# The order of the nodes worked out inside the loop over h, and x of layers 2 and 3 turned by VectorE and transfers instead of TensorE

## Chip, cores and metric

The kernel runs on one core of one Trainium2 chip. The metric is the device time of an execution in microseconds. A core has five engines that run side by side and wait for each other through semaphores: TensorE (PE; PEld is its weight load), VectorE (DVE), ScalarE (ACT), GpSimd (POOL) and SyncE (SP). SyncE computes nothing; it issues transfers (DMAs). POOL and ACT can issue them too. Each engine executes its queue in order.

## What is computed

Four graph layers run in a row over x of 8 batches, 2048 nodes and 64 features, each followed by a residual sum and a layernorm. All matrices `adj` are the same 2048 x 2048 matrix.

```
x = layernorm(x + L0(x, H, adj))   # attention over 64 hyperedges, mixed with adj/deg @ (x @ W_ind)
x = layernorm(x + L1(x, adj))      # (D^-1/2 (adj + I) D^-1/2) @ x @ W.T
x = layernorm(x + L2(x, adj))      # [x, adj x, adj adj x (combined), softmax(relu(E E.T)) x]
                                   #   times weights of each node = node_embeddings @ weights_pool
x = layernorm(x + L3(x, adj))      # three steps of v = W2 relu(W1 [v, adj v] + b1) + b2
```

The order in which nodes are visited in layer 0 is internal: nodes are sorted by the number of hyperedges they belong to, so that a tile of 128 nodes needs as few slots as possible. Every output must come out in the original order.

## The kernel before

Line numbers are those of the kernel before. The program is built with a scheduler: the source gives the instructions in a program order, and the scheduler places them on the engines by what is ready and by priority, and adds all waits. Instructions wrapped in `keep_in_program_order` (all matmuls by `mm`, all transposes by `transpose`, and those wrapped in `pin`) may not move ahead of what stands before them on their engine. A tile of a pool with a tag and `bufs` buffers waits until the oldest tile of that tag has been released by all its readers.

The four batch pairs (p = 0 to 3) are treated one after the other. x is kept as 16 tiles of 128 nodes with 128 columns (two batches of 64 features). A chunk c is 512 nodes, four tiles. N is 2048, P is 128, JT is 4, NCH is 4, NP is 4.

**Start and loop over h (lines 412 to 621).** From the hyperedge matrix the degree of each node is taken, then its rank (lines 481 to 514), and the ranks are inverted into `order`, the list of nodes for each place (lines 535 to 567): comparisons on DVE, 16 small matmuls into `po`, two DVE instructions. After that the loop over 16 tiles t (line 576) multiplies x by the first weights (`ph`, line 579), forms exponentials on ACT and products `st` and `ex` on DVE, stores `st` to `hs_hbm` every second tile, and adds up `pagg` (line 614). `fetch_rows` (line 256) gathers rows of `hs_hbm` by `order` on GpSimd's queue after the loop.

**Slots, with filler (lines 643 to 785).** The attention of layer 0 is worked out tile by tile. In between, `fill(n)` takes n matmuls from a generator `filler`, here `products()` (line 323), which multiplies x by `adj`. Inside it, `inverses()` (line 340) turns the degrees of `adj` into reciprocals. It gives way 8 times (line 351) before it starts the transposes that spread them. Each matmul of the filler advances a clock by `tick()`; `later(n, f)` and `after(n, f)` run f after n ticks.

**Mixing (lines 848 to 1040).** For 16 steps i (pair and chunk), in each pass of the loop: `mix_scores(i)`, `mix_end(i - 1)`, `mix_load(i + 2)`, `mix_ind(i + 1)`, `mix_g(i + 1)`, `mix_weigh(i)`, with 8 or 9 fills between. `mix_g` (line 864) loads the attention result `gn` and x into `rs[i]` (tag r, two buffers), transposes `gn` on TensorE, and 8 ticks later GpSimd adds `gn` to x (line 879). `mix_end` (line 913) adds the mixed part, normalizes with `normalized` and stores the result to `x1_hbm` from the same buffer `r`. The filler is now layer 1, whose inputs `l1_parts` loads from `x1_hbm`.

**Softmax of the embeddings (lines 1105 to 1170).** `ua` matmuls over all pairs.

**Layer 2 (lines 1196 to 1353).** The generator `supports()` (line 1207) computes adj x (k = 1, `u1_hbm`) and adj adj x (k = 2) for each pair in two halves g of two chunks. In the half k = 1, g = 0, after each chunk, `turned_x(p, q)` (line 1196) transposes the four tiles of x on TensorE into PSUM, ACT copies them to a buffer `ut`, and SyncE stores it to `xt_hbm`. Then GpSimd adds the bias into x. `natural` transposes u1 back for k = 2. `load_xg` (line 1287) loads `xt_hbm` and the three others, and the main loop multiplies them by the pooled weights (`py`, line 1335), DVE forms products and sums (lines 1339 and 1340), and two filler matmuls of `supports()` follow each.

**Layer 3 (lines 1319 to 1517).** v is kept transposed in `h[c]` (tags g0 to g3 and w0 to w3, by turns). `first_h(p, c, h)` (line 1295) transposes four tiles of x on TensorE and copies them to h by ACT. `factor` (line 1306) multiplies h by a weight and splits the product into two parts, which the matmuls with `adj` use. For pair 0, `first` is called inside the last passes of layer 2's loop (line 1344, `first(j - 1, 2)` for j = 1, 2) and after it (line 1360, ticks `4 * c`); for later pairs `prepare` (line 1474) calls `first_h` during the last step of the pair before.

Buffers of tag `ut` in pool `va` (two of them) serve `ut`, `raw`, `inv`, `bias`, `src`, `ar` and the squares of a layernorm.

Of the kernel before, what the change touches and what calls it, by code (L numbers as in the profile page):

```python
# [56 lines left out]
def tile_gnn_fast(  # L57
# [27 lines left out]
    P = 128  # L85
# [237 lines left out]
    def products():  # L323
# [16 lines left out]
        def inverses():  # L340

            pdc = places["small"]([P, JT, P], "pdc")
            for j in range(JT):
                transpose(pdc[:, j, :], deg4[:, cols(j, P)])
            pdc = pdc.rearrange("p j (c r) -> p c j r", c=NCH)[:, :, :, 0]
            d1 = deg1.rearrange("p (c j) -> p c j", c=NCH)
            nc.vector.tensor_scalar(d1, pdc, 1.0, None, op0=ALU.add)
            nc.gpsimd.tensor_tensor(dinv, deg1, neg_half[:, :NT], ALU.pow)
            nc.vector.tensor_scalar(d1, pdc, 1.0, None, op0=ALU.max)
            nc.vector.reciprocal(deg1, deg1)  # L350
            for _ in range(8):
                yield
            for c in range(NCH):
                pt = places["small"]([P, C], "pinv")
                for j in range(JT):
                    k = c * JT + j
                    transpose(pt[:, cols(j, P)], deg1[:, k:k + 1].to_broadcast([P, P]))
                row = va.tile([P, C], F32, tag="ut", name="inv", bufs=2)
                nc.scalar.copy(row, pt)
                nc.sync.dma_start(inv_hbm[:, cols(c)], row)  # L360
                for _ in range(4):
                    yield
# [53 lines left out]
    with tc.tile_pool(name="pa_ps", bufs=1, space=PSUM) as pps:  # L416
# [108 lines left out]
        for t in range(NT // 2):  # L525
# [5 lines left out]
        slot = pa.tile([P, NT, E], BF16, name="slot")  # L531
        nc.vector.tensor_tensor(slot, pcm, m_n, ALU.mult)


        tl = so.tile([P, NT], F32, name="tl")
        ge = so.tile([P, NT, NT], F32, name="ge")
        nc.vector.tensor_scalar(over[:, 0:NT], iota[:, 0:NT], float(P), -0.5, op0=ALU.mult, op1=ALU.add)
        wide = [P, NT, NT]
        nc.vector.tensor_tensor(
            ge, rank[:, :, None].to_broadcast(wide), over[:, None, 0:NT].to_broadcast(wide), ALU.is_gt  # L540
        )
        nc.vector.tensor_reduce(tl, ge, AX.X, ALU.add)
        nc.vector.tensor_scalar(tl, tl, -1.0, None, op0=ALU.add)
        q = so.tile([P, NT], F32, name="q")
        nc.vector.scalar_tensor_tensor(q, tl, -float(P), rank, op0=ALU.mult, op1=ALU.add)
        nc.vector.tensor_tensor(
            ge, tl[:, :, None].to_broadcast(wide), iota[:, None, 0:NT].to_broadcast(wide), ALU.is_equal
        )
        val = so.tile([P, NT, 2, NT], BF16, name="val")
        nc.vector.tensor_tensor(  # L550
            val[:, :, 0, :], ge, iota[:, 0:NT, None].to_broadcast(wide), ALU.mult
        )
        nc.vector.tensor_scalar(val[:, :, 1, :], ge, row, None, op0=ALU.mult)
        po = pps.tile([P, 2, NT], F32, tag="sm", name="po", bufs=2)
        ohq = so.tile([P, NT, P], BF16, name="ohq")
        nc.vector.tensor_tensor(
            ohq, q[:, :, None].to_broadcast([P, NT, P]), iota[:, None, :].to_broadcast([P, NT, P]), ALU.is_equal
        )
        for t in range(NT):
            nc.tensor.matmul(  # L560
                po.rearrange("p i t -> p (i t)"), lhsT=ohq[:, t, :],
                rhs=val[:, t].rearrange("p i t -> p (i t)"), start=t == 0, stop=t == NT - 1,
            )
        olo = so.tile([P, NT], F32, name="olo")
        nc.vector.tensor_copy(olo, po[:, 1, :])

        nc.vector.scalar_tensor_tensor(order, olo, float(NT), po[:, 0, :], op0=ALU.mult, op1=ALU.add)

        so_scope.close()


        seen = pa.tile([P, NT, B, 2], F32, name="seen")
# [3 lines left out]
        for t in range(NT):  # L576
            ph = pph.tile([P, 2, C], F32, tag="ph", name="ph", bufs=2)
            for p in range(NP):
                nc.tensor.matmul(
                    ph[:, p // 2, (p % 2) * 2 * (F + 2):(p % 2 + 1) * 2 * (F + 2)], lhsT=xt[t][:, p, :],  # L580
                    rhs=bd66.rearrange("p b f -> p (b f)"), start=True, stop=True,
                )
            fetch_xt(t + 2 * XB)
            hv = ph[:, :, 0:G * (F + 2)].rearrange("p k (g c) -> p k g c", c=F + 2)
            if t % 2 == 0:
                st2 = pa.tile([P, 2, HROW], F32, tag="st", name="st", bufs=3)
            st = st2[:, t % 2]
            ex = pa.tile([P, 2, G, F + 1], F32, tag="ex", name="ex", bufs=2)
            sv = seen[:, t].rearrange("p (k g) c -> p k g c", k=2)
            nc.vector.tensor_scalar(  # L590
                sv, hv[:, :, :, F:F + 2], CLIP, -CLIP, op0=ALU.min, op1=ALU.max
            )
            nc.gpsimd.tensor_copy(st[:, BF + 8:], slot[:, t, :])
            e_gn = st[:, BF:BF + 8]
            nc.scalar.activation(e_gn.rearrange("p (k g) -> p k g", k=2), sv[:, :, :, 1], AF.Exp)
            lr = pa.tile([P, B], F32, tag="lr", name="lr", bufs=2)
            nc.vector.scalar_tensor_tensor(
                lr, seen[:, t, :, 0], 0.2, seen[:, t, :, 0], op0=ALU.mult, op1=ALU.max
            )
            tc.keep_in_program_order(  # L600
                nc.scalar.activation(ex[:, :, :, F], lr.rearrange("p (k g) -> p k g", k=2), AF.Exp)
            )
            for k in range(2):
                nc.vector.scalar_tensor_tensor(
                    st[:, k * G * F:(k + 1) * G * F].rearrange("p (g f) -> p g f", f=F), hv[:, k, :, 0:F], 1.0,
                    e_gn[:, k * G:(k + 1) * G, None].to_broadcast([P, G, F]), op0=ALU.add, op1=ALU.mult,
                )
            nc.vector.tensor_tensor(
                ex[:, :, :, 0:F], hv[:, :, :, 0:F], ex[:, :, :, F:F + 1].to_broadcast([P, 2, G, F]), ALU.mult
            )  # L610
            if t % 2:
                nc.scalar.dma_start(hs_hbm.rearrange("(p t) c -> p t c", t=NT)[:, t - 1:t + 1, :], st2)
            for k in range(2):
                nc.tensor.matmul(
                    pagg[k * E:(k + 1) * E, 0:G * (F + 1)], lhsT=m_n[:, t, :], rhs=ex[:, k].rearrange("p g c -> p (g c)"),
                    start=t == 0, stop=t == NT - 1,
                )
            if t in paced:
                behind(seen[:, t, 0, 0:1])
                load_adj(paced[t], 0)  # L620
            if t in (9, 11):
                parts(0, (t - 9) // 2)
# [185 lines left out]
    def wide(c):  # L808
        return slice(c * JT, (c + 1) * JT)

    uts, invs, gts, inds, tts, rs = {}, {}, {}, {}, {}, {}
    xn, done, stored, due = [], [0] * NP, set(), set()


# [49 lines left out]
    def mix_g(i):  # L864
# [3 lines left out]
        nc.sync.dma_start(  # L868
            gn, gs_hbm.rearrange("(p t) f -> p t f", t=NT)[:, wide(c), p * P:(p + 1) * P]
        )  # L870
        rs[i] = mp.tile([P, JT, P], F32, tag="r", name="r", bufs=2)
        load_x(rs[i], p, c)
        pg = lps.tile([P, C], F32, tag="mm", name="pg", bufs=4)
        for j in range(JT):
            transpose(pg[:, cols(j, P)], gn[:, j, :])
        gts[i] = mp.tile([P, C], F32, tag="gt", name="gt", bufs=2)
        pin(nc.scalar.activation(gts[i], pg, AF.Identity, bias=-1.0))
        r = rs[i]
        after(8, lambda: pin(nc.gpsimd.tensor_tensor(r, r, gn, ALU.add)))

    def mix_scores(i):

# [14 lines left out]

        pin(nc.gpsimd.tensor_tensor(inds[i], inds[i], gts[i], ALU.subtract))
        after(5, differences)

    def mix_weigh(i):

# [10 lines left out]
    def mix_end(i):  # L913
# [5 lines left out]

        def end():  # L920
            nc.sync.dma_start(x1_hbm[p][:, wide(c), :], r)
            stored.add((p, c))
            if p == 0:
                first_parts(c, mixed)
# [94 lines left out]
    mix_load(1)  # L1019
    fill(24)  # L1020
    mix_ind(0)
    fill(12)
    mix_g(0)
    fill(4)
    for i in range(steps + 1):
        k = 9 if i > NCH else 8
# [162 lines left out]
    def natural(c, ut):  # L1189
# [3 lines left out]
            transpose(pn[:, j, :], ut[:, cols(j, P)])  # L1193
        x_part[c] = split(va, pn, f"v{c}", 1, [P, JT, P])

    def turned_x(p, c):
        pt = lps.tile([P, C], F32, tag="mm", name="pt", bufs=4)
        for j in range(JT):
            transpose(pt[:, cols(j, P)], xn[p][:, c * JT + j, :])
        out_t(xt_hbm[p], c, pt, nc.scalar)  # L1200

        bias = l2.tile([P, JT, 1, F], F32, tag="bias", name="bias", bufs=1)
        nc.sync.dma_start(bias[:, :, 0, :], bias_hbm[:, wide(c), :])
# [90 lines left out]

    def first_h(p, c, h):

        pt = lps.tile([P, C], F32, tag="mm", name="pt", bufs=4)
        for j in range(JT):
            transpose(pt[:, cols(j, P)], xn[p][:, c * JT + j, :])
        nc.scalar.copy(h, pt)  # L1300
        if c == 0:

            nc.vector.tensor_copy(h[:, 0:1], ivc)
# [22 lines left out]
    for p in range(NP):  # L1326
        for c in range(NCH):
            r = staged("r").rearrange("p t (b f) -> p t b f", f=F)
            for b in range(2):
                a_z = xg[b]  # L1330
                for j in range(JT):
                    e_b = emb_n[:, c * JT + j:c * JT + j + 1, :].to_broadcast([P, OH, D])
                    for k in range(2):
# [5 lines left out]
                        nc.vector.tensor_tensor(pr, py, e_b, ALU.mult)  # L1339
                        nc.vector.tensor_reduce(r[:, j, b, cols(k, OH)], pr, AX.X, ALU.add)  # L1340
                        fill(2)
                    if p == NP - 1 and c == NCH - 1 and b == 1 and j in (1, 2):

                        first(j - 1, 2)
                if c + 1 < NCH:
                    load_xg(p, c + 1, b)
                elif p + 1 < NP:
# [9 lines left out]

    STEPS = 3
    for c in (2, 3):
        first(c, 4 * c)  # L1360
    bd_v2 = l2.tile([P, P], F32, name="bd_v2")
    rows = l2.tile([P, 2, P], F32, tag="e", name="rows")
    more = l2.tile([P, 2, P], F32, tag="bias", name="more")
# [888 lines left out]
```

## Time and profile before

| | us |
|---|---|
| median of 11 runs | 1967.83 (1963.46 to 1975.41) |
| the profiled execution's own time | 1964.94 |
| its span, first to last instruction | 1963.1 |
| mean granted TensorE clock | 0.982 |
| transfers | 143.10 MB, mean 73 GB/s |

In the profile an instruction line has the engine, the line of the source, the operation, the tiles written and read (out<-in), the shape and the count. "busy" is the union of their times. "idle before" is the time for which the engine stood still just ahead of them, with what ended it behind an arrow. A line that is a helper's (L171 for `mm`, L174 for `transpose`, L167 for `split`) is shared by many places, so tiles tell them apart. In the chain of waits, time is followed back from the last instruction to what released each one. An `SPq` line is a transfer issued on SyncE's queue; the three durations of such a row are its least, median and largest issue time in ns.

### The profile page before, as it was taken

The page shows a single profiled execution, that of the slowest core. Times are in us where ns is not written, and L with a number is a line of the kernel's source. Part 1 is how long each engine was busy: PE and PEld are TensorE (multiplying, and loading weights), DVE is VectorE, ACT ScalarE, POOL GpSimd, SP SyncE. Part 2 cuts the span into 40 slices and gives each one's busy share as a digit, 9 for nine tenths or more (in the row PEclk, how much of TensorE's full clock was granted, in tenths as well). Part 3 has the DMA queues.
Part 4 walks back from the last instruction along what each step waited for, and adds up shares of the span by engine and source line. Part 5 has one row for each costly group of instructions (what it writes and reads, how often), then busy time and mean ns, then how long its engine had stood idle before and what let it go on. Part 6 is the DMA issues. An engine that isn't in the chain of part 4 may idle for free.

```text
span 1963.1 us, 19567 instructions
## 1 busy us (share of the span) xinstructions
PE 1872.1 (95%) x7100; PEld 1214.8 (62%) x7100; DVE 1001.1 (51%) x1741; ACT 393.1 (20%) x771; POOL 529.8 (27%) x480
## 2 busy tenths in 40 slices
PE   6889799888999999999999999999999999999997
PEld 4667565555744444855655575566447787877875
DVE  7779655565632221356556736755785343343332
ACT  1455343233222121100000000000002222222211
POOL 3678654454454434211000101100001020100201
PEclk9999999899999999999999999999999999999999
DMA  9823343332500000311101111111111122121211
GB/s 313 307 96 99 124 133 124 120 117 81 185 6 27 27 1 22 119 38 59 57 31 36 57 51 33 56 47 35 43 33 38 38 56 54 44 54 49 54 27 24
DMA packets 94186, 143.10 MB, mean 73 GB/s; under 512 B 29233, under 2 KB 40113, under 8 KB 93697
## 3 DMA queue, kind: packets, MB, share of 16 engines
q1 hardware_dynamic: 83920, 105.39, 17.8%
q0 software_dynamic: 7760, 27.66, 4.3%
q10 hardware_dynamic: 2400, 8.72, 1.2%
q8 instruction: 58, 0.95, 0.2%
q14 instruction: 48, 0.39, 0.1%
HBM read 98.67 MB, written 43.06 MB: 72 GB/s over the span
## 4 chain that ended last, share of the span: by engine, by line
PE 76%; DMA 4%; DVE 4%; POOL 3%; issue 2%; ACT 1%; SPq 0%; POOLq 0%; DVEq 0%; ACTq 0%
PE u L171 33%; PE py L171 22%; PE ua L171 11%; PE ug L171 2%; PE pr L171 2%; DMA r<-in_x_n 1%; DMA x_hbm<-r 1%; POOL ln_r L839 1%; PE po L171 1%; PE pt L174 1%; PE s L171 1%; PE pf L171 1%; DVE r L842 0%; DMA gs_hbm<-acc,order 0%; POOL y L944 0%
## 5 line engine op out<-in xcount | busy, mean ns | idle before, releaser
L171 PE MATMUL py<-wp,xg 128*128 128x512 f32 x1024 | 475.2, 592 | 0.5 <-DMA xg<-u_hbm 0.5
L171 PEld LDWEIGHTS py<-wp,xg 128*128 128x128 f32 x1024 | 193.3, 189 | 161.2 <-issue 138.5
L1339 DVE TENSOR_TENSOR fcav<-py,emb_n 128x512 f32<-128x512 f32 x256 | 176.9, 691 | 134.9 <-PE py L171 129.2
L171 PE MATMUL ua<-pt,xn 128*128 128x512 f32 x512 | 230.2, 592 | 1.6 <-DVE pt L1120 1.6
L1340 DVE TENSOR_REDUCE r<-fcav 128x32 f32<-128x512 f32 x256 | 175.6, 686 | 8.2
L171 PEld LDWEIGHTS ua<-pt,xn 128*128 128x128 f32 x512 | 96.9, 190 | 111.2 <-issue 104.2
L154 POOL TENSOR_TENSOR ln_r<-ln_e,neg_half 128x8 f32<-128x8 f32 x32 | 53.5, 1672 | 400.1 <-DVE ln_e L152 369.7
L171 PE MATMUL u<-adj,v0h 128*128 128x512 f32 x384 | 149.1, 456 | 1.3 <-ACT h L1495 1.3
L171 PE MATMUL u<-adj,v2l 128*128 128x512 f32 x384 | 140.8, 431 | 2.3 <-DVE v2l L167 2.3
L171 PE MATMUL u<-adj,v2h 128*128 128x512 f32 x384 | 141.6, 435 | 0.0
L171 PE MATMUL u<-adj,v1h 128*128 128x512 f32 x384 | 140.6, 433 | 0.0
L171 PE MATMUL u<-adj,v0l 128*128 128x512 f32 x384 | 140.3, 432 | 0.0
L171 PE MATMUL u<-adj,v3l 128*128 128x512 f32 x384 | 139.7, 429 | 0.0
L171 PE MATMUL u<-adj,v3h 128*128 128x512 f32 x384 | 138.6, 428 | 0.0
L171 PE MATMUL u<-adj,v1l 128*128 128x512 f32 x384 | 138.5, 427 | 0.0
L1120 DVE TENSOR_SCALAR pt<-pt 128x512 f32<-128x512 f32 x64 | 30.2, 473 | 150.3 <-ACT pt L1119 150.2
L1126 POOL TENSOR_TENSOR acc<-acc,pt 128x512 f32<-128x512 f32 x60 | 76.5, 1275 | 107.1 <-DVE pt L1120 106.5
L1421 DVE SCALAR_TENSOR_TENSOR ar<-fcav,ar 128x512 f32<-128x512 f32 x64 | 45.7, 715 | 108.8 <-ACT ar L1420 108.8
L171 PEld LDWEIGHTS u<-adj,v0h 128*128 128x128 f32 x384 | 71.7, 191 | 37.8 <-issue 24.9
L171 PEld LDWEIGHTS u<-adj,v2l 128*128 128x128 f32 x384 | 72.8, 191 | 32.7 <-issue 15.7
L171 PEld LDWEIGHTS u<-adj,v3l 128*128 128x128 f32 x384 | 72.6, 190 | 30.3 <-issue 15.7
L171 PEld LDWEIGHTS u<-adj,v1l 128*128 128x128 f32 x384 | 72.6, 190 | 29.2 <-issue 14.4
(360 smaller groups left out, 2719.9 us busy)
## 6 DMA issues: line engine op xcount, KB each, us to landing
adj<-in_adj_t POOLq DMA_DIRECT2D x32, 512.0 KB, 8.1
fcav<-in_adj_t SPq DMA_DIRECT2D x64, 256.0 KB, 2.9
u_hbm<-ut SPq DMA_DIRECT2D x48, 256.0 KB, 2.4
xg<-u_hbm SPq DMA_DIRECT2D x96, 128.0 KB, 2.9
x_hbm<-r SPq DMA_DIRECT2D x28, 256.0 KB, 2.1
hs_hbm<-st ACTq DMA_DIRECT2D x8, 584.0 KB, 5.4
xt<-in_x_t SPq DMA_DIRECT2D x16, 256.0 KB, 5.5
ut<-u_hbm SPq DMA_DIRECT2D x16, 256.0 KB, 3.3
```

Of the source, the lines that this page charges most:

```text
L154: nc.gpsimd.tensor_tensor(rstd, vare, neg_half[:, :groups], ALU.pow)
L171: tc.keep_in_program_order(nc.tensor.matmul(*args, **kw))
L174: tc.keep_in_program_order(nc.tensor.transpose(dst, src, ident))
L839: pin(nc.gpsimd.tensor_tensor(rstd, vare, neg_half[:, :groups], ALU.pow))
L1120: nc.vector.tensor_scalar(pt, pt, 1.0, None, op0=ALU.max)
L1126: nc.gpsimd.tensor_tensor(accs[c], accs[c], pt, ALU.add)
L1339: nc.vector.tensor_tensor(pr, py, e_b, ALU.mult)
L1340: nc.vector.tensor_reduce(r[:, j, b, cols(k, OH)], pr, AX.X, ALU.add)
L1421: nc.vector.scalar_tensor_tensor(ar.bitcast(F32), seen_a, 1.0, ar.bitcast(F32), op0=ALU.mult, op1=ALU.not_equal, accum_out=left[:, t, k:k ...
```

## The change

Five edits are made together.

1. `inverses()` gives way 20 times instead of 8.
2. The lines that invert the ranks into `order` become a function `place()`, called in the loop over h at t == 9, after that tile's `ex`. Its first instruction is pinned to its place in the program. The pool `so` is closed at its end.
3. In mixing, the load of x and its buffer leave `mix_g`. `mix_x(i)` makes them: twice ahead of the loop, then for step i + 2 as soon as step i's result has been given to its store. GpSimd's sum is traced by `mix_scores`. The fills ahead of the first `mix_g` become 28 instead of 12.
4. `turned_x` and `first_h` call `turn`: DVE transposes all 32x32 squares of four tiles at once into a buffer `squares` of tag `ut`, and 16 transfers on SyncE's queue put the squares into place, in `xt_hbm` or in h.
5. `first` is called for c = 0 and 1 after j == 0, with 5 and 6 ticks, and for c = 2 and 3 with 20 and 25 ticks (before: after j == 1 and 2 with 2 ticks, then 8 and 12).

```diff
-            for _ in range(8):
+            for _ in range(20):
                 yield
...
+        def place():
+            tl = so.tile([P, NT], F32, name="tl")
+            ge = so.tile([P, NT, NT], F32, name="ge")
+            tc.keep_in_program_order(
+                nc.vector.tensor_scalar(over[:, 0:NT], iota[:, 0:NT], float(P), -0.5, op0=ALU.mult, op1=ALU.add)
+            )
...
+            so_scope.close()
...
+            if t == 9:
+                place()
             if t % 2:
...
-        rs[i] = mp.tile([P, JT, P], F32, tag="r", name="r", bufs=2)
-        load_x(rs[i], p, c)
+        gns[i] = gn
...
-        r = rs[i]
-        after(8, lambda: pin(nc.gpsimd.tensor_tensor(r, r, gn, ALU.add)))
+
+    def mix_x(i):
+        if i < steps:
+            rs[i] = mp.tile([P, JT, P], F32, tag="r", name="r", bufs=2)
+            load_x(rs[i], *divmod(i, NCH))
...
         after(5, differences)
+        r, gn = rs[i], gns.pop(i)
+        after(8, lambda: pin(nc.gpsimd.tensor_tensor(r, r, gn, ALU.add)))
...
             nc.sync.dma_start(x1_hbm[p][:, wide(c), :], r)
+            mix_x(i + 2)
...
-    fill(12)
+    fill(28)
     mix_g(0)
+    mix_x(0)
+    mix_x(1)
...
+    def turn(p, c, dst):
+        S = 32
+        squares = va.tile([P, C], F32, tag="ut", name="squares", bufs=2)
+        nc.vector.transpose(squares, xn[p][:, wide(c), :].rearrange("p t f -> p (t f)"))
+        dst = dst.rearrange("(m r) (j i q) -> i m r j q", r=S, i=P // S, q=S)
+        for i in range(P // S):
+            src = squares[i * S:(i + 1) * S, :].rearrange("r (j m q) -> m r j q", j=JT, q=S)
+            for m in range(P // S):
+                nc.sync.dma_start(dst[i, m], src[m])
+
     def turned_x(p, c):
-        pt = lps.tile([P, C], F32, tag="mm", name="pt", bufs=4)
-        for j in range(JT):
-            transpose(pt[:, cols(j, P)], xn[p][:, c * JT + j, :])
-        out_t(xt_hbm[p], c, pt, nc.scalar)
+        turn(p, c, xt_hbm[p][:, cols(c)])
...
     def first_h(p, c, h):
-        pt = lps.tile([P, C], F32, tag="mm", name="pt", bufs=4)
-        for j in range(JT):
-            transpose(pt[:, cols(j, P)], xn[p][:, c * JT + j, :])
-        nc.scalar.copy(h, pt)
+        turn(p, c, h)
...
-                    if p == NP - 1 and c == NCH - 1 and b == 1 and j in (1, 2):
-                        first(j - 1, 2)
+                    if p == NP - 1 and c == NCH - 1 and b == 1 and j == 0:
+                        first(0, 5)
+                        first(1, 6)
...
-        first(c, 4 * c)
+        first(c, 10 + 5 * c)
```

More of the change, by code (lines that the diff above doesn't have):

```diff
@@ L532, in tile_gnn_fast @@
         nc.vector.tensor_tensor(slot, pcm, m_n, ALU.mult)
[L535 to L562, printed above, removed]
-            )
@@ L564, in tile_gnn_fast @@
[L564 to L569, printed above, removed]
+        def place():
[3 more added lines that the diff above has]
+                nc.vector.tensor_scalar(over[:, 0:NT], iota[:, 0:NT], float(P), -0.5, op0=ALU.mult, op1=ALU.add)
+            )
+            wide = [P, NT, NT]
+            nc.vector.tensor_tensor(
+                ge, rank[:, :, None].to_broadcast(wide), over[:, None, 0:NT].to_broadcast(wide), ALU.is_gt
+            )
+            nc.vector.tensor_reduce(tl, ge, AX.X, ALU.add)
+            nc.vector.tensor_scalar(tl, tl, -1.0, None, op0=ALU.add)
+            q = so.tile([P, NT], F32, name="q")
+            nc.vector.scalar_tensor_tensor(q, tl, -float(P), rank, op0=ALU.mult, op1=ALU.add)
+            nc.vector.tensor_tensor(
+                ge, tl[:, :, None].to_broadcast(wide), iota[:, None, 0:NT].to_broadcast(wide), ALU.is_equal
+            )
+            val = so.tile([P, NT, 2, NT], BF16, name="val")
+            nc.vector.tensor_tensor(
+                val[:, :, 0, :], ge, iota[:, 0:NT, None].to_broadcast(wide), ALU.mult
+            )
+            nc.vector.tensor_scalar(val[:, :, 1, :], ge, row, None, op0=ALU.mult)
+            po = pps.tile([P, 2, NT], F32, tag="sm", name="po", bufs=2)
+            ohq = so.tile([P, NT, P], BF16, name="ohq")
+            nc.vector.tensor_tensor(
+                ohq, q[:, :, None].to_broadcast([P, NT, P]), iota[:, None, :].to_broadcast([P, NT, P]), ALU.is_equal
+            )
+            for t in range(NT):
+                nc.tensor.matmul(
+                    po.rearrange("p i t -> p (i t)"), lhsT=ohq[:, t, :],
+                    rhs=val[:, t].rearrange("p i t -> p (i t)"), start=t == 0, stop=t == NT - 1,
+                )
+            olo = so.tile([P, NT], F32, name="olo")
+            nc.vector.tensor_copy(olo, po[:, 1, :])
+            nc.vector.scalar_tensor_tensor(order, olo, float(NT), po[:, 0, :], op0=ALU.mult, op1=ALU.add)
+            so_scope.close()
@@ L809, in wide @@
         return slice(c * JT, (c + 1) * JT)
-    uts, invs, gts, inds, tts, rs = {}, {}, {}, {}, {}, {}
+    uts, invs, gts, gns, inds, tts, rs = {}, {}, {}, {}, {}, {}, {}
     xn, done, stored, due = [], [0] * NP, set(), set()
```

## The prediction

> **What bounds the kernel now.** I read the busy table first, then the busy share of the forty slices, then windows cut where the stages change, then what ends TensorE's idle time, then the chain of waits and the timelines at the edited places.
>
> ```profile
> PE 1872.1 (95%) x7100; PEld 1214.8 (62%) x7100; DVE 1001.1 (51%) x1741; ACT 393.1 (20%) x771; POOL 529.8 (27%) x480
> PE   6889799888999999999999999999999999999997
> ...
> 0.00:190.00 190.00, 154.32 (x750) 116.00 (x751) 147.56 (x320) 79.08 (x220) 123.36 (x171) 0.94 0.62 208
> 238.00:505.00 267.00, 238.51 (x1012) 154.25 (x1013) 149.71 (x220) 90.84 (x158) 129.72 (x103) 0.95 0.38 119
> 841.00:1482.00 641.00, 641.00 (x1957) 358.28 (x1956) 403.14 (x604) 39.71 (x67) 53.90 (x38) 1.00 0.13 43
> 1494.00:1963.00 469.00, 452.37 (x2132) 360.33 (x2132) 163.43 (x365) 95.69 (x160) 45.82 (x29) 0.99 0.18 45
> ```
>
> In a window line the columns are length, then the busy us of PE, PEld, DVE, ACT and POOL, granted clock, DMA share, GB/s. TensorE sets the end: in layer 2 (841 to 1482) it has no idle time, so what leaves TensorE there is gained in full, and what makes it wait there is lost in full. Two stretches have room: the start (36 us idle of 190) and the mixing stage (28.5 us idle of 267). The waits say why the second is idle: three lines on GpSimd and TensorE over 238 to 545 and 300 to 545, and one step of the chain of waits (start, length, what).
>
> ```profile
> POOL r L879 <- DMA r<-in_x_n: 66.6, 12, 7.5
> ...
> PE po L171 <- ACT ut L1007: 9.7, 3, 7.0
> PE pf L171 <- DVE ind L862: 5.3, 4, 3.1
> ...
> 335.73 0.70 DVE r L842
> 336.45 2.87 DMA x_hbm<-r
> 339.38 3.65 DMA r<-in_x_n
> 343.15 1.30 POOL r L879
> ```
>
> Each mixing step stores its result r, waits for the landing, loads x into the freed buffer, and GpSimd stands still until that has landed, 12 times for 5.5 us on the mean. Queued behind it on GpSimd are the subtraction L898, the scaling of layer 1's input L944 and the powers L839; DVE and ACT wait for those, TensorE for DVE and ACT.
>
> [...] No run here shows the instruction. [...] The trace agrees that the data are cheap: DMA share is 0.13 in layer 2. It is SyncE's issue that I count.
>
> **The change part by part.** All sums are made in the profiled execution, span 1963.1 us.
>
> *A, order inside the loop.* Between 13.5 and 20.6 us the block puts 11 instructions of 5.2 us on DVE (the largest, ohq, 2.28), and TensorE waits 3.5 us for val. Moved to the tenth tile, its first instruction pinned, they meet a loop in which DVE waits six times, 6 us in all, between 39.6 and 55.9. The 16 small matmuls (0.6 us) and the two PSUM reads move along; no DMA is in the block, and `order` is first used by the gather at 58.3, which waits for the last store of hs anyway. Gain: at most the 3.5 us. But the DMA share is 0.78 to 1.09 until 50 us, so the stores of st may take the place of the wait. If the DVE gaps don't coincide, the 5.2 us fall on the loop. I take -1, from -4 to +5.
>
> *B, 20 yields instead of 8.* TensorE waited 2.9 us for the reciprocal behind a power of 2.95 us on GpSimd. Twelve matmuls at 0.235 us are 2.8 us of work put in front. DVE's own stop of 4.7 us for that power stays. -2, from 0 to -3.
>
> *C, x of a step loaded when step i-2 has been stored; the sum L879 moved from mix_g to after mix_scores.* The load and its wait for the store stay on SyncE's queue. A step is 32 ticks in 16.7 us, 0.52 us a tick. In a pass of the loop the store of step i is issued at tick 25, and the sum for step i+2, whose x goes into the same buffer, stood at tick 24. Now it stands at tick 8 of the next pass, 15 ticks or 7.8 us after the issue. Store and load need 5 to 6.5 us in the chain. So the 66.6 us on GpSimd nearly go. What is late next is TensorE itself: 278 us busy out of 307 between 238 and 545. Also 28 fills instead of 12 before the first mix_g put 3.7 us of matmuls over a 5.3 us wait for gn. TensorE's waits in 238 to 545 sum to 31 us (5.3 for gn, 25.7 behind it); I take 20 of them as gained, because the waits for tanh and for layer 1's first parts have other causes too. Bounds 0 and -29.
>
> *D, TensorE's turning of x goes.* It is 32 groups of four transposes, half in layer 2 and half in layer 3.
>
> ```profile
> L174 PE MATMUL pt<-ident,xn 128*128 128x128 f32 x128 | 18.0, 272 | 0.0
> ...
> 792.50 0.63 PE L171 MATMUL u<-adj,v3l 128*128 128x512 f32 x2
> 792.97 0.60 PE L174 MATMUL pt<-ident,xn 128*128 128x128 f32 x4
> ```
>
> A chunk with its group repeats in 4.18 us and holds eight pairs of 0.467, so a group is worth 0.445 us: 32 of them 14.2 us, on the path. The ACT copies (32 of 0.59) go too and were hidden. GpSimd's sums into x (L1205, L1392) then wait for DVE's square instead.
>
> *E, what replaces it.* Each turn is one DVE instruction of 0.69 us (32 make 22 us; DVE is 63% busy in layer 2 and 35% in layer 3, so hidden) and 16 transfers of 32 partitions by four runs of 128 bytes, all on SyncE's queue. Such an issue is not in the trace. The nearest rows: 0.32 us for 128 whole rows, 0.395 for out_x in 256-byte runs, and for 64 partitions
>
> ```profile
> L1292 SPq DMA_DIRECT2D xg<-u_hbm x96: 444/572/1014, 804.8 to 1452.4; - x96
> L1292 SPq DMA_DIRECT2D xg<-xt_hbm x32: 444/445/451, 812.7 to 1450.6; - x32
> ```
>
> I bound it by 0.32 and 0.57 and take 0.445: 7.1 us of queue a turn, 228 us in all, plus 2.3 us for the last landing. For that time a buffer of tag ut (two in all, shared with u's copies, src, ar and the layernorm) is held.
>
> Where can this be seen? (1) Pair 0 in layer 2 has four turns in 16 us of matmuls, and two ut buffers must come free for u1, whose transposes stand on TensorE's queue at 812.95 and 817.12. SyncE issues other loads until 802.4. (2) The start of layer 3: tags g0 and g1 are freed at about 1467, when the last b=0 ends, g2 and g3 at the end. Turns land in a row, h[1] at 1483.6 and h[3] at 1497.6 where `factor` on TensorE's queue wants them at 1478.4 and 1492.7: +10, less the 2.3 us wait that stood there, +8. (3) Pairs 1 to 3 in layer 2: a chunk lasts 10.7 us, longer than a turn; a DVE copy of u queued behind a held buffer delays the products behind it, and TensorE with four PSUM buffers: +2. (4) In layer 3 the next pair's h[2] and h[3] are prepared some 29 and 42 ticks (6.7 and 9.7 us) before their factor.
>
> For (1) and (4) it matters how early the turn is issued. It is not pinned, and its x is ready long before. The trace shows that such instructions do move ahead:
>
> ```profile
> 1574.55 2.54 POOL L1392 TENSOR_TENSOR xn<-xn,rows 128x512 f32<-128x512 f32 x2 [79.44 <-PE pt L174]
> ```
>
> This sum for pair 1 belongs in the code behind pair 0's last step, which ends about 1603. The ut buffers are idle from about 750 to 784 and the other tag of h is free a step ahead. So I take half of (1) as issued ahead: +4, and (4) as covered but for ut: +3. E is 8+4+2+3 = +17, from +3 (0.32 and all ahead) to +77 (0.57 and none ahead).
>
> Sum: -1-2-20-14+17 = -20: span 1943. The profiled execution's own time was 1.8 us above its span, and 2.9 us below the median of the runs: 1948.
>
> **Rivals.** *Strong gain:* turns wholly hidden (E +3) and the mixing stage full (-26): -40, at 1928. For it: all data of a turn exist early. Against: at the start of layer 3 the buffers don't. *Wash:* GpSimd's 66 us give way to another wait of the same chain (SyncE stands behind the same store; C -5), and E eats D: about -4 to +4, at 1966. For it: the store's landing stays in the queue; against: the 7.8 us. *Slower, by SyncE's queue:* turns stay at their place in the code. With 0.445 us an issue, (1) stops TensorE 17 us, because u1's copies wait for the third and fourth turn; (2) 8; (4) 7 for each of three pairs; 47 against gains of 37, +10. With 0.57 it is 26, 16 and 35, 77 in all, +40. The middle, near 0.48, is about +20: 1988. It decides as soon as these stops exceed 37 us, which is at some 0.4 us an issue with nothing ahead. For it: SyncE is in order and its stores of u and loads of xg stand behind 16 issues each. Against: the sums of L1392.
>
> **How the numbers follow.** Forecast 0.50, at 1948, its own range 1936 to 1960. Strong gain 0.17, wash 0.09, slower 0.24. Leaving out the ends of the second and the last, 0.05 and 0.11, the range is 1924 to 1985. 0.2% is 4 us, about what a measurement of this kernel can tell from no change; a third of the wash is beyond it on the fast side: faster 0.70, same 0.06, slower 0.24.
>
> **What would show it.** Right: L879 waits for x under 15 us in all; TensorE's idle time in mixing falls below 12 us; layer 2 from the first py to the last is shorter by about 5 us. Issues of a turn near 0.45 us. Wrong: TensorE idle before the pn transposes of pair 0 or before pr at the start of layer 3 and at each change of pair, with SyncE busy all the while; a `po` wait at the old size in mixing; DVE's copies of u waiting for transfers of a turn.

## The result and the profile after

Line numbers are now those of the changed kernel; the lines named in the prediction stand there as follows: L879 is L907, L1339 is L1355, L1392 is L1409, L1415 is L1432. The transfers of a turn are L1216, the squares L1211.

| | before | after |
|---|---|---|
| median us | 1969.2 (31 runs) | 2056.51 (2055.41 to 2061.16, 8 runs) |
| ratio | | 1.0445, interval 1.0429 to 1.046 |
| span of the profiled execution | 1963.1 | 2057.7 |
| mean granted clock | 0.982 | 0.96 |

The change makes the kernel slower by 4.45%; the forecast was 1948, faster. The page of the changed kernel: busy times, TensorE's forty slices, the counts of transfers, the chain by engine and by line, and the group of `factor`'s matmuls.

```profile
PE 1873.3 (91%) x6972; PEld 1212.0 (59%) x6972; DVE 1023.9 (50%) x1773; ACT 376.8 (18%) x739; POOL 531.0 (26%) x480
PE   6888999998999996999999999999789599698697
...
DMA packets 165613, 147.36 MB, mean 72 GB/s; under 512 B 102704, under 2 KB 113584, under 8 KB 165120
...
PE 16%; SPq 6%; DMA 1%; DVE 1%; issue 1%; POOL 1%; ACT 0%; POOLq 0%; ACTq 0%; DVEq 0%
PE u L171 14%; SPq L1216 6%; PE pr L171 2%; DMA fcav<-in_adj_t 1%; POOL ln_r L154 1%; PE po L171 0%; DVE r L155 0%; DMA h<-squares 0%; DVE ar L1438 0%; DVE ln_v L150 0%; ACT ar L1437 0%; SPq L1419 0%; DVE src L1330 0%; DVE r L1416 0%; ACT h L1512 0%
...
L171 PE MATMUL pr<-bd_e,h 128*128 128x128 f32 x128 | 26.4, 372 | 90.0 <-DMA h<-squares 90.0
```

TensorE has no full row of nines in the last quarter any more, and in the chain of work that ended last an issue queue (SPq L1216, the turns' transfers) appears with 6% of the span. (The shares of this chain add up to 26%: it goes back to 1510.6 us only, so it speaks for layer 3.) `factor`'s 128 matmuls have 90 us of idle time ahead of them, all of it put down to the transfers of h.

Where the time went is read by cutting both traces at the same events: the last copy of the raw softmax messages (DVE raw), the first product of layer 2 (DVE fcav), the last residual sum of layer 2, the end. Each row is one stage of the profiled executions, in us. The columns behind "after" are experiments described below, and all of them hold edits 1 to 3.

| stage | before | after | edits 1-3 alone | x turned only | h turned only | two queues | h earlier | x of pairs 1-3 only |
|---|---|---|---|---|---|---|---|---|
| to the last raw copy | 785.0 | 756.8 | 755.1 | 756.0 | 755.7 | 756.1 | 756.3 | 752.2 |
| pair 0 of layer 2's products | 55.9 | 79.6 | 56.5 | 78.9 | 57.0 | 67.1 | 77.2 | 56.3 |
| rest of layer 2 | 641.3 | 636.4 | 641.3 | 636.1 | 641.6 | 637.0 | 636.4 | 636.1 |
| layer 3 | 480.9 | 584.9 | 479.8 | 481.4 | 585.8 | 504.9 | 524.6 | 480.5 |
| span | 1963.1 | 2057.7 | 1932.7 | 1952.4 | 2040.1 | 1965.1 | 1994.5 | 1925.1 |

The first half gains 28 us. Pair 0 loses 24, layer 3 loses 104, and the 4.9 us that the rest of layer 2 gains are nearly the 12 groups of transposes at 0.445 us that left TensorE there. The waits of the changed kernel that carry the loss (us in all, times, longest), and its instructions with the tile `squares` (count, then least, median and largest ns, first and last start):

```profile
PE pr L171 <- DMA h<-squares: 90.0, 12, 18.6
...
ACT ut L1192 <- DMA xt_hbm<-squares: 42.6, 1, 42.6
...
PE pn L174 <- ACT ut L1192: 16.9, 1, 16.9
```

```profile
L1216 SPq DMA_DIRECT2D xt_hbm<-squares x256: 303/430/1836, 774.3 to 1271.2; - x128
L1216 SPq DMA_DIRECT2D h<-squares x256: 585/599/1495, 1454.6 to 1923.8; - x128
L1211 DVE STREAM_TRANSPOSE squares<-xn x32: 689/703/714, 768.6 to 1898.2; 128x512 f32<-128x512 f32 x32
...
DMA to landing us min/median/max: 1.5/1.8/3.5
```

The square costs what was forecast: 0.70 us, where the forecast's 0.69 was its author's estimate after the 128x512 TENSOR_REDUCE L1340 of the kernel before (686 ns on the mean). The transfer doesn't: 0.43 us of SyncE when it goes to HBM, 0.60 when it goes to SBUF. And the turns are not ahead of their place. SyncE's timeline at pair 0, at the start of layer 3 and at the first change of pair (start, length, what, count):

```profile
774.32 7.65 SPq L1216 DMA_DIRECT2D xt_hbm<-squares  x16
...
1454.65 42.60 SPq L1216 DMA_DIRECT2D h<-squares  x64
...
1578.84 1.33 SPq L1216 DMA_DIRECT2D h<-squares  x2
1581.23 0.33 SPq L1432 DMA_DIRECT2D fcav<-in_adj_t  x1
1581.62 19.36 SPq L1216 DMA_DIRECT2D h<-squares  x30
1601.07 4.88 SPq L1432 DMA_DIRECT2D fcav<-in_adj_t  x2
1608.95 4.56 SPq L1419 DMA_DIRECT2D out_x<-r  x4
1613.61 21.98 SPq L1216 DMA_DIRECT2D h<-squares  x32
```

64 issues to SBUF take 42.60 us without a gap, so a turn of h is 10.65 us of queue, against 7.1 in the forecast. The queue is solid with issues there, while the data are little work: in these 42.6 us the DMA share is 0.16, and a transfer of a turn lands 1.8 us after its issue (median of all turns).

At the change of pair the four turns, and what stands between them, hold the queue from 1578.8 to 1635.6, and TensorE gets the last h at 1637.1. Between the second turn and the third lie 12.6 us. The chain of waits says what fills them (start, length, what):

```profile
1600.38 0.60 SPq L1216
1601.07 3.09 DMA fcav<-in_adj_t
1604.24 0.63 ACT ar L1437
...
1610.82 1.75 DVE r L155
1613.61 0.59 SPq L1216
```

Layer 3 also loads `adj` once more, block by block (fcav), and checks it. Such a load had stood behind the first two turns. ScalarE waits for it in order (6.55 us of idle time ahead of this `ar`), and the layernorms of pair 0's results r are queued behind it, the first at 1604.77; SyncE then waits for these, which it stores (out_x), before it comes to the third turn. So the queue's delay comes back to the queue. TensorE's timeline at the same place shows a second cost:

```profile
1625.79 2.05 PE L171 MATMUL pr<-bd_e,h 128*128 128x128 f32 x8 [18.61 <-DMA h<-squares]
...
1628.06 1.05 PE L171 MATMUL u<-adj,v3h 128*128 128x512 f32 x2
1628.91 1.05 PE L171 MATMUL u<-adj,v3l 128*128 128x512 f32 x2
...
1631.42 0.63 PE L171 MATMUL u<-adj,v3h 128*128 128x512 f32 x2
1631.89 0.63 PE L171 MATMUL u<-adj,v3l 128*128 128x512 f32 x2
1637.08 2.05 PE L171 MATMUL pr<-bd_e,h 128*128 128x128 f32 x8 [4.56 <-DMA h<-squares]
```

After the stop of 18.61 us the same matmuls take 1.05 instead of 0.63 us for some 5 us. Three windows of the same execution, just before the stop, over it and just behind it; the granted clock is the number behind the five busy times:

```profile
1602.00:1608.00 6.00, 4.88 (x24) 3.82 (x24) 2.06 (x5) 2.26 (x4) 1.46 (x1) 1.00 0.33 86
1608.00:1626.00 18.00, 0.21 (x1) 0.24 (x2) 4.33 (x6) 0.28 (x1) 4.32 (x4) 0.58 0.23 45
1626.00:1631.00 5.00, 5.00 (x16) 4.27 (x17) 1.39 (x3) 0.93 (x2) 0.00 (x0) 0.50 0.15 23
```

The clock is 0.50 just after the stop, against 1.00 before it. Full speed (pairs of `u` at 0.62 to 0.63 us, granted clock 1.00) is back 5.6 us after this stop, and 5.0 and 3.0 us after those of 7.23 and 8.06 us at the start of layer 3. Which stops have a lower clock behind them is taken up in the last section.

### The profile page after: what moved, and what is told of

Read it like the earlier page. It is cut to its first block, busy times and chain, and to the rows that moved or that the text cites. A ratio compares the mean times of both kernels' runs of the same rounds, so it can differ in the third digit from the quotient of the medians.

```text
span 2057.7 us, 20022 instructions
## 1 busy us (share of the span) xinstructions
PE 1873.3 (91%) x6972; PEld 1212.0 (59%) x6972; DVE 1023.9 (50%) x1773; ACT 376.8 (18%) x739; POOL 531.0 (26%) x480
## 5 line engine op out<-in xcount | busy, mean ns | idle before, releaser
L1355 DVE TENSOR_TENSOR fcav<-py,emb_n 128x512 f32<-128x512 f32 x256 | 176.7, 690 | 122.3 <-PE py L171 115.7
L171 PE MATMUL pr<-bd_e,h 128*128 128x128 f32 x128 | 26.4, 372 | 90.0 <-DMA h<-squares 90.0
L171 PEld LDWEIGHTS u<-adj,v3h 128*128 128x128 f32 x384 | 73.9, 193 | 29.9 <-issue 15.0
```

The source lines that it names most:

```text
L171: tc.keep_in_program_order(nc.tensor.matmul(*args, **kw))
```

## The experiments

**First set: which part does what.** Theory: the loss is the queue of issues of the turns, and edits 1 to 3 are a gain of their own. Rivals: edits 1 to 3 share in the loss, or layer 3 inherits its loss from layer 2.

Edits 1 to 3 alone (`turned_x` and `first_h` as before; edit 5, which belongs to `first_h`, is taken back too):

```diff
-        turn(p, c, xt_hbm[p][:, cols(c)])
+        pt = lps.tile([P, C], F32, tag="mm", name="pt", bufs=4)
+        for j in range(JT):
+            transpose(pt[:, cols(j, P)], xn[p][:, c * JT + j, :])
+        out_t(xt_hbm[p], c, pt, nc.scalar)
...
-        turn(p, c, h)
+        pt = lps.tile([P, C], F32, tag="mm", name="pt", bufs=4)
+        for j in range(JT):
+            transpose(pt[:, cols(j, P)], xn[p][:, c * JT + j, :])
+        nc.scalar.copy(h, pt)
```

> Edits 1 to 3 alone: the order, the yields and the mixing as in the changed kernel, but both turns on TensorE as before. Theory 'issue queue' (the loss is all in the turns' transfers, and the two traces show the last raw copies of the messages 28 us earlier): about 28 us faster than before, some 1941 us, ratio 0.984 to 0.989. Rival 'interaction' (the earlier mixing pushes other loads into layer 2 and 3, so that edits 1 to 3 bring part of the loss): 1965 us or more.

Measured: 1935.14 us against 1967.18, ratio 0.9847 (0.9816 to 0.9879). Edits 1 to 3 gain 32 us and carry none of the loss.

The two turns alone (edits 4 and 5), put into the kernel before:

> The kernel before with the two turns alone put on VectorE and transfers. Theory 'issue queue': layer 2 +19 us, layer 3 +104 us, so about 2092 us, ratio 1.055 to 1.070. Rival 'interaction': at most 2070 us, since the mixing's stalls of the kernel before leave the queue time to catch up.

Measured: 2086.78 us, 1.061 (1.058 to 1.064), that is +119.6. Together with the -32.0 of the other part it makes +87.6; the whole change is +87.3. The parts add.

The changed kernel with only `first_h` and edit 5 taken back (x turned by squares in layer 2), and with only `turned_x` taken back (h turned by squares in layer 3). Edit 5 has no run of its own; it stands wherever all of h is turned by squares:

> The changed kernel with the turn of h in layer 3 back on TensorE; x of layer 2 still turned by VectorE and 16 transfers a turn. Theory 'issue queue': -28 of edits 1 to 3, +19 of layer 2's turns: about 1960 us, ratio 0.992 to 0.999. Rival (layer 2's turns delay what layer 3 needs too): 1980 us or more.

> The changed kernel with the turn of x in layer 2 back on TensorE; h of layer 3 still turned by VectorE and transfers. Theory 'issue queue': -28 of edits 1 to 3, +104 of layer 3's turns: about 2040 us, ratio 1.030 to 1.045. Rival (the loss in layer 3 is inherited from layer 2's turns): below 2000 us.

Measured: 1954.33 us, 0.9924 (0.9902 to 0.9947), and 2039.71 us, 1.0367 (1.0339 to 1.0395). Against edits 1 to 3 alone that is +19 for x and +105 for h. The stage table shows each loss in its own stage, with the other stages as without the turns. Layer 3's loss in these two traces, windows over the whole of layer 3, first edits 1 to 3 alone, then h turned by squares:

```profile
1452.90:1932.70 479.80, 462.62 (x2189) 368.05 (x2187) 170.70 (x377) 98.74 (x167) 52.31 (x33) 0.99 0.18 45
```

```profile
1454.30:2040.10 585.80, 481.48 (x2146) 378.33 (x2146) 178.66 (x389) 92.86 (x153) 49.33 (x33) 0.91 0.19 43
```

TensorE's idle time grows from 17.2 to 104.3 us, and its busy time by 18.9, although 51 of the 64 single transposes that are gone (0.111 us each, 5.7 in all) stood in this window; one group of `factor`'s matmuls (0.9 us) has come into it. So by this estimate about 24 of the 106 us are matmuls at the lower clock behind stops.

**Second set: is it the issue, or the buffers and the landing?** The squares also wait for two `ut` buffers shared with a layernorm, and a turn must land; both would delay h without any queue. Three edits of the changed kernel.

Every second transfer of a turn on ScalarE's queue, buffers and bytes the same:

```diff
-                nc.sync.dma_start(dst[i, m], src[m])
+                (nc.scalar if m % 2 else nc.sync).dma_start(dst[i, m], src[m])
```

> The changed kernel, with every second transfer of a turn issued by ScalarE's queue instead of SyncE's; all else the same. Theory 'issue queue' (a turn is late by the time in which one queue issues 16 transfers one after the other): the eight of a queue take about half of that, so the visible part of the 127 us falls by half or more: about 1990 us, between 1970 and 2010. Rival 'buffers' (the squares wait for a ut buffer, or the landing or the transpose itself is late): 2040 us or more.

Measured: 1966.56 us, 0.9989 (0.9973 to 1.0005), 3 us below the range given: 90 of the 121 us that the turns cost are gone. Its tile `squares` (`ACTq` is a transfer issued on ScalarE's queue) and the wait of `factor`:

```profile
L1216 SPq DMA_DIRECT2D h<-squares x128: 585/600/1438, 1441.5 to 1832.8; - x128
L1216 ACTq DMA_DIRECT2D h<-squares x128: 592/612/1731, 1441.5 to 1830.2; - x128
```

```profile
PE pr L171 <- DMA h<-squares: 24.3, 6, 8.1
```

Both queues issue side by side at nearly the pace of one (0.600 and 0.612 us an issue; the first 16 in a row take ScalarE 10.87 us, against 10.65 for SyncE alone in the changed kernel), so the issue is limited by the queue far more than by anything that the queues share. Shorter stops also cost less clock: with 24.3 us in six stops of `factor` instead of 90.0 in twelve, the granted clock over the run is 0.979 instead of 0.96.

Every transfer issued twice, the same bytes to the same place:

```diff
-            for m in range(P // S):
+            for m in list(range(P // S)) * 2:
```

> The changed kernel, with every transfer of a turn issued twice (the same bytes to the same place), so 32 issues a turn. Theory 'issue queue': 9.6 us more for each of 16 turns of h and 7.5 us for each of 16 turns of x, of which in pairs 1 to 3 of layer 2 much stays covered: +180 us, between +150 and +260, so some 2240 us. Rival 'buffers' or 'landing': less than +60, below 2120 us.

Measured: 2264.28 us, 1.1503 (1.1464 to 1.1541): +208 against the changed kernel, in the range of the queue and far from the rival's bound of +60. The wait of `factor`, in which twice the issues make 2.7 times the stop:

```profile
PE pr L171 <- DMA h<-squares: 245.4, 16, 25.4
```

Both edits also change how long a turn holds its `ut` buffer. They rule out buffers or landings that are late whatever the number of issues in a row, but not a buffer that is late because the issues take long. In pair 0 of layer 2 that is the very way to TensorE (ScalarE's copy `ut` above). At the start of layer 3 the 64 issues follow without a gap, so no square came late for them. At the changes of pair no run parts the two.

The turns of h for the next pair taken up a step of layer 3 earlier, into buffers that are free by then; the four turns at the start of layer 3 as in the changed kernel:

```diff
-                if last and p + 1 < NP:
-                    for c in own:
+                if step == 1 and p + 1 < NP:
+                    for k, c in enumerate(own):
                         def prepare(c=c):
-                            h_next[c] = first_h(p + 1, c, new_h(c))
-                        later(2 if g else 40, prepare)
+                            hn = l2.tile([P, C], F32, tag=f"w{c}", name=f"h{c}")
+                            h_next[c] = first_h(p + 1, c, hn)
+                        later(20 + 60 * k, prepare)
...
                     for k, c in enumerate(mine):
+                        if last and p + 1 < NP:
+                            place[c] = "w"
                         h[c] = new_h(c)
```

> The changed kernel, with the turns of h for the next pair of samples taken up one step of layer 3 earlier (in step 1 instead of the last; the buffer is free then); the four turns at the start of layer 3 stay as they are. Theory 'issue queue, and too late in it': at the three changes of pair the stalls of about 22 us each go, 66 in all, less what the loads of the adjacency check lose behind the turns: about 2000 us, between 1990 and 2025. Rival (the queue has no room for them anywhere, or the stall is the buffers'): 2045 us or more.

Measured: 1995.61 us, 1.0138 (1.0104 to 1.0172), -61 against the changed kernel. `factor` waits only at the start of layer 3 any more. From the first result of layer 3 to the last it takes 377.4 instead of 451.8 us, but up to the first result 134.4 instead of 120.7. A part comes back as a new wait of TensorE. The waits, and one such place in ScalarE's and in TensorE's timeline:

```profile
PE u L171 <- ACT v2h L166: 19.3, 3, 8.0
PE pr L171 <- DMA h<-squares: 17.9, 3, 8.1
```

```profile
1584.24 0.62 ACT L1437 CAST ar<-fcav 128x512 fp32r<-128x512 f32 x1 [10.44 <-DMA fcav<-in_adj_t]
```

```profile
1588.07 1.22 PE L171 MATMUL u<-adj,v2h 128*128 128x512 f32 x2 [7.96 <-ACT v2h L166]
```

The load of the check (fcav) is issued behind 16 transfers of a turn, and ScalarE waits for it in order. VectorE's comparison with it, the sum `src` and then `v2h`, which TensorE needs, stand behind that. VectorE stands still as well until a transfer of an earlier turn of h has landed, before it can make the next squares: 25.5 us in five stops over the run.

So the place in the queue decides too: with the same 16 issues a turn, most of what the changes of pair cost is gone.

**A version in between.** Edits 1 to 3, and only x of pairs 1 to 3 by squares (pair 0 and layer 3 on TensorE):

```diff
-        turn(p, c, xt_hbm[p][:, cols(c)])
+        if p:
+            turn(p, c, xt_hbm[p][:, cols(c)])
+        else:
...
+            out_t(xt_hbm[p], c, pt, nc.scalar)
```

> Edits 1 to 3, both turns on TensorE, except x of pairs 1 to 3 in layer 2, which VectorE and the transfers turn. Theory 'issue queue': only pair 0 waits for its turns (+24 us there), the others are covered and save 12 x 0.445 us of TensorE: about 5 us faster than edits 1 to 3 alone, 1930 us, ratio 0.979 to 0.984. Rival (the transfers delay the loads of layer 2 in the other pairs too): 1938 us or more.

Measured: 1931.12 us, 0.9814 (0.9788 to 0.9841). The rest of layer 2 is 5.2 us shorter in the trace, as forecast, and no engine waits for the tile `squares` at all. Against edits 1 to 3 alone the intervals overlap; it is the fastest median of all, not a proven step.

**Third set: which of edits 1 to 3, and can h be covered too?** Each edit alone in the kernel before:

> The kernel before with edit 3 alone: x of the mixing loaded a step or two ahead by the end of a step, its sum with gn taken later, 28 fills ahead. The forecast's part C, enlarged by what edits 1 to 3 gave together (-32): about -24 us, 1944 us, ratio 0.983 to 0.992. Rival (the order's place or the yields gave most of it): -12 us or less, ratio above 0.994.

> The kernel before with edit 2 alone: the order of the nodes worked out inside the loop over h, at its tenth tile. The forecast's part A: -4 to +5 us; with what edits 1 to 3 gave together about -5 us, ratio 0.995 to 1.000. Rival (it is the order's place that opens the time for the mixing): -12 us or more, ratio below 0.994.

> The kernel before with edit 1 alone: 20 yields in place of 8 between the reciprocal of the degrees and its transposes. The forecast's part B: -2 us (0 to -3), ratio 0.997 to 1.001. Rival: more than 5 us either way.

Measured: 1939.13 us, 0.9847 (0.9831 to 0.9864); 1967.23, 0.9999 (0.9988 to 1.001); 1966.45, 0.9994 (0.9983 to 1.0004). The mixing gives all that can be measured. How, is seen in windows from 238 us to the first matmul of the stage behind the mixing (`pb`), before and then after:

```profile
238.00:511.30 273.30, 244.81 (x1039) 159.40 (x1039) 153.25 (x228) 92.67 (x161) 129.72 (x103) 0.94 0.38 121
```

```profile
238.00:483.30 245.30, 232.06 (x1039) 152.63 (x1040) 162.63 (x234) 93.74 (x162) 137.74 (x107) 1.00 0.43 139
```

The same number of matmuls, 28.0 us earlier: 15.3 of it idle time (28.5 to 13.2), and 12.7 shorter matmuls at a granted clock of 1.00 instead of 0.94. This split is that of two executions; from 238 to 490 us, with the start of the next stage in it, the clock is 0.98 in the changed kernel and 0.97 with edits 1 to 3 alone. In the changed kernel GpSimd still waits 24.6 us for x in this part, in eight waits, and TensorE 5.3 us for a load ahead of `pb`, which it now reaches too early:

```profile
POOL r L907 <- DMA r<-in_x_n: 24.6, 8, 5.3
...
PE pb L171 <- DMA xn<-in_emb: 5.3, 1, 5.3
```

The version in between, and h of pairs 1 to 3 by squares a step earlier, on two queues:

```diff
-        turn(p, c, h)
+        if p:
+            turn(p, c, h, nc.scalar)
+        else:
...
+            nc.scalar.copy(h, pt)
...
-                nc.sync.dma_start(dst[i, m], src[m])
+                (other if m % 2 else nc.sync).dma_start(dst[i, m], src[m])
```

> Edits 1 to 3; pair 0 of both turns on TensorE; x of pairs 1 to 3 by squares and SyncE; h of pairs 1 to 3 by squares, one step of layer 3 earlier, its transfers alternating between SyncE's and ScalarE's queues. Theory 'issue queue': all turns left on VectorE are covered, TensorE is spared 24 x 0.445 us = 11 us against edits 1 to 3 alone, so about 1925 us, ratio 0.976 to 0.981. Rival (what the issues take from ScalarE and from the loads of the check costs more than they spare): 1936 us or more, ratio above 0.983.

Measured: 1943.12 us, 0.9865 (0.9846 to 0.9883), a miss: the rival holds. Layer 3 takes 492.1 us instead of 480.5. No matmul waits for a turn of h any more, but TensorE waits 9.5 us in three places for `v2h` of ScalarE. One of them, in ScalarE's and TensorE's timelines:

```profile
1537.15 5.16 ACTq L1216 DMA_DIRECT2D h<-squares  x8
1542.36 0.62 ACT L166 CAST v2h<-src 128x512 fp32r<-128x512 f32 x1 [4.68 <-DMA h<-squares]
```

```profile
1543.03 0.73 PE L171 MATMUL u<-adj,v2h 128*128 128x512 f32 x2 [2.67 <-ACT v2h L166]
```

The cast starts when ScalarE has issued the last of eight transfers that stand ahead of it: half a turn, 5.16 us of queue, is on the path again, on another engine.

## Why the prediction failed

**The step that failed is E**, and in it the sentence on which (1) and (4) rest: that turns would be issued ahead of their place because the sums of L1392 had been. Those sums stand on GpSimd, which had nothing else to do (79.44 us of idle time ahead of the one for pair 1). The turns stand on SyncE, in order with everything else, and the timeline has them in a row where the code has them. The second error is the price: 0.445 us an issue, taken from loads of 64 partitions out of HBM and bounded at 0.57; from SBUF to SBUF an issue costs 0.60, and with the gap behind it 0.67. The signs that the prediction had named for being wrong came: TensorE stood before `pn` of pair 0 and before `pr` at the start of layer 3 and at each change of pair, with turns on SyncE's queue. By terms:

- (1) pair 0 of layer 2: +4 forecast, +23.7 measured (16.9 of it one stop of TensorE behind ScalarE's copy of u1, ahead of which ScalarE stood idle for 42.6 us, until a transfer of a turn had landed and its buffer was free). The rival's 17 for this place was right for the idle time.
- (2) the start of layer 3: +8 forecast. From the last sum of layer 2 to the first result of layer 3 it takes 120.7 instead of 103.8 us: +17.
- (3) pairs 1 to 3 of layer 2: +2 forecast, nothing seen. The stage became 4.9 us shorter, where D alone had forecast 12 x 0.445 = 5.3.
- (4) the changes of pair: +3 forecast; from the first result of layer 3 to the last 451.8 instead of 364.7 us: +87, or 29 for each change. The rival with nothing ahead and 0.57 had 12 a change. Two turns in a row need 21 us of queue and then land, where 6.7 and 9.7 us were to be had; and the third turn began 12.6 us after the second had ended, behind the load, the layernorms and the stores shown above. Its square started on VectorE only at 1608.91, and the fourth at 1612.48; how much of this is the `ut` buffers, which the layernorms use too, stays open.

E was to cost 17. The two turns cost 121 us between edits 1 to 3 alone and the whole change, which already holds what D gained, 14 if the forecast was right there, so E cost about 135. The rival "slower, by SyncE's queue" had the mechanism, the places and the order of events; its 1988 was 69 us too low because of the price, because of (4), and because it counted idle time alone and no lower clock behind the stops (0.50 in the window above; about 24 us in layer 3 by the estimate).

**C was right, and too small.** -20 forecast, -28 measured. TensorE's idle time in mixing fell to 13.2 us, or 7.9 without the wait ahead of `pb`, which is new (forecast: under 12). The waits of L879 fell from 66.6 to 24.6, not under 15; none of TensorE's own waits there is put down to them. Of idle time 15.3 us went, less than the 20 forecast; the 12.7 us on top are matmuls at a higher clock, which the forecast left out. **A** and **B** (-1 and -2) are within what can be measured. **D** fits where it can be seen, 4.9 against 5.3 us in the rest of layer 2, less whatever (3) cost there.

## What to carry to other kernels

Price a transpose by squares in issues: 16 small transfers for 0.445 us of TensorE are some 7.5 to 10.7 us of a queue here. In these runs they were free in pairs 1 to 3 of layer 2 alone, where no engine waited for the squares and the stage became 5.2 us shorter. That an instruction could start early says nothing of one on another queue; ask of each queue what stands in it at that moment. And count a stop of TensorE at more than its length, whether it is saved or added: in mixing, where 15.3 us of stops went, the granted clock rose from 0.94 to 1.00, and in layer 3 of the changed kernel all eight stops of 4.13 us or more had a clock of 0.50 behind them, and two of the shorter ones 0.62 and 0.59. By the estimate of 24 us above, that is 2 to 3 us on top of each of these ten stops (the estimate is from the trace with h alone turned by squares, where TensorE waits for h 89.8 us in 12 stops, against 90.0 in 12 here).

## What had not been expected of the hardware

- The issue of one and the same small transfer out of SBUF (32 partitions, four runs of 128 bytes) takes 0.43 us to HBM and 0.60 to SBUF, and SyncE's and ScalarE's queues do it side by side at nearly the same pace (0.600 and 0.612 us to SBUF). The issue is most of the cost here, 10.65 us a turn beside 1.8 us to landing, and the second queue is worth 90 us (2056.51 to 1966.56).
- Which stops lower the clock is not told by their length alone. In layer 3 of the changed kernel the granted clock was 0.50 over the first 1.8 us behind every stop of 4.13 us and more: the eight matmuls of `factor` took 2.04 to 2.05 us, against 1.05 to 1.06 without a stop in the kernel before. Of the shorter stops of `factor`, those of 1.72 and 2.13 us left them near full speed (1.13 us, clock 1.00), but those of 1.89 and 2.06 us slowed them to 1.73 and 1.82 (clock 0.62 and 0.59), and the next pairs of `u` to 1.05 from 0.63. No run shows what sets the two kinds apart. From TensorE's timeline:

```profile
1488.37 1.13 PE L171 MATMUL pr<-bd_e,h 128*128 128x128 f32 x8 [2.13 <-DMA h<-squares]
...
1747.04 1.73 PE L171 MATMUL pr<-bd_e,h 128*128 128x128 f32 x8 [1.89 <-DMA h<-squares]
...
1748.99 1.05 PE L171 MATMUL u<-adj,v2h 128*128 128x512 f32 x2
```
